# Layer 0's rows go back to their own order through a DRAM scratch and an accumulating indirect transfer

## The chip, the cores and the metric

The kernel runs on one core of a Trainium2 chip. The metric is the time of one execution on the device in microseconds (us), the median of several runs. Profiles come from one execution each.

## The reference

There are 128 graphs of 128 nodes with 64 features each, in float32, and two layers. `L0` and `L1` are the two networks below, and both layers use the same weighted adjacency:

```python
def L0(x, adj, W1, b1, W2, b2):
    mask = (adj > 0.0).astype(x.dtype)
    W1a, W1b = W1[:F], W1[F:]                    # F = 64, H = 192
    diff = x[:, :, None, :] - x[:, None, :, :]
    h = relu((x @ W1a)[:, :, None, :] + diff @ W1b + b1)
    hm = einsum('bjkh,bjk->bjh', h, mask)
    return hm @ W2 + mask.sum(-1)[..., None] * b2

def L1(feat, adj, W1, b1, W2, b2, W3, b3):
    agg = einsum('bmn,bnd->bmd', adj, feat)
    h = elu(agg @ W1 + b1)
    h = elu(h @ W2 + b2)
    return h @ W3 + b3

x = layernorm(x + L0(x, adj, ...))
x = layernorm(x + L1(x, adj, ...))
```

## The kernel before

**Tiling.** Two graphs make a pair, and there are 64 pairs (`NP`). Partitions are the 128 nodes, or 2 × 64 hidden channels of the two graphs. The adjacency has few entries in a row, so the kernel does not form all 128 × 128 differences. For each graph it ranks the nodes by the number of neighbours they have (`prepare`: `mk` is the mask, `pos` the rank of each node, `permb` the permutation matrix of it). It puts x into that sorted order with a matmul (`sort_x`) and also the mask (`sort_mask`). Then nine blocks of nodes (`BLOCKS`), each with a fixed number of neighbour slots, are worked off: in each unit ACT copies the node's own term `aj` into a PSUM bank `e` (L910), PE adds the neighbours' terms by 18 matmuls of one-hot matrices `oh` with `cp` (L920), and DVE sums absolute values over the slots into `sums` (L930). Four banks `e` are used in turn.

**The end of a pair** (`finish`). POOL forms `hm` from `sums` and a correction `corr` (L842). PE multiplies by W2 and adds the linear terms (L847, L851). ACT copies the result, in sorted order, to SBUF as `ys` (L855). PE brings the rows back to their own order by two float32 matmuls with the transposed permutation `permT` (L864). `permT` has been made in `sort_mask` by two matmuls of `permb` with an identity (L246, in the same PSUM bank as the sorted mask) and a copy on ACT (L661). Then `norm` adds x on DVE (`y`, L737), takes bn_stats (`st`, L742), makes the factors on POOL (`ve`, `rs`, `nb`, L749 to L753) and applies them on ACT to give `x1` (L771). Layer 1 follows: the product with the adjacency (L871), two hidden layers with elu on ACT and DVE (L791 to L797, L880, L886), the last matmul (L893), a second `norm` and the store of the output by SP (L897).

**What sets the order.** No engine's order is left to a scheduler at run time. All steps of all pairs are generators, and a small planner (`Flow`) calls them in the order of due times, which are written out by hand in a table `DUE`, in us of a plan with one round (one pair) per 11.1651 us. The entry of pair p is due at `ROUND * p` plus its number in the table. While the plan is under way, the step with the earliest due time is always issued next:

```python
            if self.under_way:
                t, th = min(ready, key=lambda r: self._rank(r[1]))
```

So the instructions of several pairs are interleaved in a fixed order on each engine. Waits are semaphores that the framework places where one engine uses what another has made.

Of the kernel before, what the change touches and what calls it, by code (L numbers as in the profile page):

```python
# [31 lines left out]
F32 = mybir.dt.float32  # L32
BF16 = mybir.dt.bfloat16
I32 = mybir.dt.int32
AF = mybir.ActivationFunctionType
OP = mybir.AluOpType
# [10 lines left out]
@with_exitstack  # L47
def gnn_kernel(ctx: ExitStack, tc: tile.TileContext, x, adj, w1, b1, w2, b2,
               v1, c1, v2, c2, v3, c3, out):
    nc = tc.nc  # L50
    B, N, F = x.shape
    H = w1.shape[1]
    O = w2.shape[1]
    H1 = v1.shape[1]
    P = 128
    HB = H // 3
    assert N == P and 2 * F == P and 2 * HB == P and H == 3 * HB and H1 == P and O == F and B % 4 == 0
    NP = B // 2

    LAY, E = [], 0  # L60
    for p0, p1, s in BLOCKS:
        n = s * (p1 - p0)
        assert 3 * n <= 512
        LAY.append((E, n, p0, p1, s))
        E += n
    NB = len(LAY)

    cpool = ctx.enter_context(tc.tile_pool(name="consts", bufs=1))
    ctx.enter_context(tc.manual_schedule())

    def const(shape, dt, name):
        return cpool.tile(shape, dt, name=name)


    degs = const([P, B], F32, "degs")

    with ExitStack() as fast:
        loads = fast.enter_context(tc.tile_pool(name="loads", bufs=8))
        prep = fast.enter_context(tc.tile_pool(name="prep", bufs=5))
        work = fast.enter_context(tc.tile_pool(name="work", bufs=5))  # L80
        ps_e = fast.enter_context(tc.tile_pool(name="ps_e", bufs=1, space=bass.MemoryType.PSUM))
        ps_m = fast.enter_context(tc.tile_pool(name="ps_m", bufs=1, space=bass.MemoryType.PSUM))
        K = sparse(tc, locals())
    with ExitStack() as slow:
        dense(tc, locals())
# [101 lines left out]
def sparse(tc, env):  # L187

    g = type("env", (), dict(env))
    nc, P, N, F, H, O, HB, H1, NP, E = (  # L190
        g.nc, g.P, g.N, g.F, g.H, g.O, g.HB, g.H1, g.NP, g.E)
    LAY, NB = g.LAY, g.NB
    loads, prep, work, ps_m = g.loads, g.prep, g.work, g.ps_m
# [3 lines left out]
    flow = Flow([ps_m.tile([P, 512], F32, name=f"m{i}") for i in range(4)])  # L197
    ADJ, XX, S = {}, {}, {}
# [3 lines left out]
    ROUND = 11.1651  # L202
    AHEAD = 4

    DUE = {
        "prepare": (-43.06, -42.93, -39.21, -39.08, -35.87),
        "sort_x": (-26.76, -10.46, -10.33, -3.14, -3.02, 2.5, 2.63, 2.76, 2.89),
        "sort_mask": (-26.12, -25.99, -25.86, -23.42, -23.29, -23.16, -13.67, -13.28, -13.03,
                      -12.77, -2.63, -2.25, -1.99, -1.73),
        "turn": (-36.9, -36.77),  # L210
        "project_c": (-32.15, -29.32, -29.2, -29.07, -28.94, -4.17, -4.04),
        "finish": (12.64, 19.44, 19.57, 21.62, 21.75, 21.88, 22.01, 28.04, 28.17, 29.2, 33.56,
                   33.69, 33.82, 34.71, 43.31, 43.44, 44.47, 44.6, 46.52, 46.65, 48.06, 48.19,
                   59.87),
        "unit": [(-1.48, 0.96, 1.09), (2.12, 2.25, 2.37), (3.02, 3.14, 3.27), (3.66, 3.79, 3.91),
# [1 line left out]
                 (7.25, 11.61, 11.74)],  # L217
    }

    def begin_thread(name, p, gen):  # L220
        flow.start(ROUND * p, DUE[name], gen)

    def event(*key):
        return EV.setdefault(key, [])

    def happened(ev, *key):
        event(*key)[:] = ev
# [5 lines left out]
    def act(n, pointers=0):  # L233
        return 0.07 + 0.09 * pointers + n / 1200

    def dve(n):
        return 0.08 + n / 960
# [12 lines left out]
    def flat(t):  # L250
        return t.rearrange("p s n -> p (s n)")
# [48 lines left out]
    rows = temp([P, NR], F32, "rows")  # L300
# [235 lines left out]
    def prepare(p):  # L536

        a = ADJ[p]
        d = S[p] = {}
        mk = d["mk"] = prep.tile([P, 2, N], BF16, name="mk")  # L540
        deg = g.degs[:, 2 * p:2 * p + 2]

        def count():
            for s in range(2):
                nc.vector.tensor_scalar(mk[:, s, :], a[:, s, :], 0.0, 0.0, op0=OP.is_gt,
                                        op1=OP.add, accum_out=deg[:, s:s + 1])
        ev, = yield ("DVE", 0.54, [event("load", p)], 0, count)
        degb = prep.tile([P, 2], BF16, name="degb")
        keyc = prep.tile([P, 2], F32, name="keyc")

        def keys():
            nc.gpsimd.tensor_copy(degb, deg)
            nc.gpsimd.tensor_sub(keyc, deg, jcol)
        ev, = yield ("POOL PORT", 0.32, [ev] + made("jcol"), 0, keys)

        def spread(key):
            for s in range(2):
                stationary(key[:, s * N:(s + 1) * N],
                           lambda h: degb[:, s:s + 1].to_broadcast([P, h.stop - h.start]),
                           identb, start=True, stop=True)  # L560
            stationary(key[:, 2 * N:3 * N], lambda h: small[:, h], iotb, start=True, stop=True)
        ev, key = yield ("PE:*", 0.17, [ev] + made("identb", "small", "iotb"), 1, spread)
        pos = prep.tile([P, 2], F32, name="pos")
        cmp = prep.tile([P, 2, N], BF16, name="cmp", bufs=3)

        def rank():
            for s in range(2):
                nc.vector.scalar_tensor_tensor(cmp[:, s, :], key[:, s * N:(s + 1) * N],
                                               keyc[:, s:s + 1], tie, op0=OP.subtract,
                                               op1=OP.is_gt, accum_out=pos[:, s:s + 1])  # L570
        ev, = yield ("DVE", 0.54, [ev] + made("tie"), 0, rank)
        permb = d["permb"] = prep.tile([P, 2, N], BF16, name="permb")

        def permute():
            nc.vector.tensor_tensor(permb, key[:, 2 * N:3 * N].rearrange("p (s n) -> p s n", s=1)
                                    .to_broadcast([P, 2, N]),
                                    pos.rearrange("p (s o) -> p s o", o=1).to_broadcast([P, 2, N]),
                                    op=OP.is_equal)
        ev, = yield ("DVE", 0.36, [ev], 0, permute)
        flow.give(key, ev)  # L580
        begin_thread("sort_x", p, sort_x(p, ev))
        begin_thread("sort_mask", p, sort_mask(p, ev))

    def sort_x(p, ev):

# [59 lines left out]
    def sort_mask(p, ev):  # L645

        d, a, permb = S[p], ADJ[p], S[p]["permb"]

        def sort(t):
            for s in range(2):  # L650
                stationary(t[:, s * N:(s + 1) * N], lambda h: d["mk"][:, s, h], permb[:, s, :],
                           start=True, stop=True)
            for s in range(2):
                stationary(t[:, (2 + s) * N:(3 + s) * N], lambda h: permb[:, s, h], identb,
                           start=True, stop=True)
        ev, t = yield ("PE:*", 0.22, [ev], 1, sort)
        mtp = d["mtp"] = prep.tile([P, 2, N], BF16, name="mtp", bufs=7)
        permT = d["permT"] = prep.tile([P, 2, N], F32, name="permT", bufs=7)
        evm, = yield ("ACT", act(2 * N), [ev], 0, lambda: nc.scalar.copy(flat(mtp), t[:, :2 * N]))
        happened(evm, "mtp", p)  # L660
        ev, = yield ("ACT", act(2 * N), [ev], 0, lambda: nc.scalar.copy(flat(permT), t[:, 2 * N:]))  # L661
        flow.give(t, ev)
        happened(ev, "permT", p)
        ev, vps = yield ("PE:*", 0.12, [evm] + made("prefix"), 1,
                         lambda vps: stationary(vps[:, :2 * N], lambda h: prefix[:, h], flat(mtp),
                                                start=True, stop=True))
        vp = prep.tile([P, 2, N], BF16, name="vp")
        ev, = yield ("ACT", act(2 * N), [ev], 0, lambda: nc.scalar.copy(flat(vp), vps[:, :2 * N]))  # L668
# [58 lines left out]
                     lambda: nc.gpsimd.tensor_sub(cp[:, 2], r1, cp[:, 1]))  # L727
        happened(ev, "cp", p)

    LATE = NP - 1  # L730

    def norm(p, yps, ev, name, rest, shift):


        y = work.tile([P, 2, O], F32, name="y", bufs=6)
        ev, = yield ("DVE", dve(2 * O), [ev], 0,
                     lambda: nc.vector.tensor_add(flat(y), yps[:, :2 * O], flat(rest)))  # L737
        flow.give(yps, ev)
        st = work.tile([P, 2, 3], F32, name="st", bufs=12)

        ev, = yield ("DVE", 0.2, [ev], 0,
# [93 lines left out]
    def finish(p):  # L835
# [19 lines left out]
        ev, = yield ("ACT", act(2 * O), [ev], 0, lambda: nc.scalar.copy(ys, yb[:, :2 * O]))  # L855
        flow.give(yb, ev)
        if p == NP - 1:
            due = DUE["finish"]
            flow.start(ROUND * p, [due[4]] * 4 + [due[8], due[12], due[12], due[14], due[15], due[15]],
                       overflow())  # L860

        def unsort(t):
            for s in range(2):
                nc.tensor.matmul(t[:, s * O:(s + 1) * O], d["permT"][:, s, :],  # L864
                                 ys[:, s * O:(s + 1) * O], start=True, stop=True)
        ev, t = yield ("PE", 0.4, [ev, event("permT", p)], 1, unsort)
        x1, ev = yield from norm(p, t, ev, "x1", xx, True)

        def aggregate(t):
# [309 lines left out]
```

## Time and profile before

| | |
|---|---|
| Median of three timed runs (lowest, highest) | 760.54 us (758.67, 761.2) |
| Span of the profiled execution, first to last instruction | 758.2 us |
| Granted TensorE clock, mean of the span | 0.988 |
| Busy share: PE, DVE, ACT, POOL | 97%, 95%, 93%, 57% |
| Matmuls L920 with the one-hot matrices | 393.3 us busy, 10368 of them |
| Matmuls L864 with `permT` | 256 passes, 275 ns median of one |
| Copies of `permT` (L661) on ACT | 64, 379 ns median of one |
| Sums `y` of layer 0 (L737) on DVE | 64, 276 ns median of one |
| First and last copy `ys` (L855) begin at | 47.5 us and 741.1 us |

The page gives the profiled execution by its span alone; the timed median is 2.3 us longer than that. Busy time counts an engine from the start of an instruction to its modelled end, and neighbouring instructions overlap by a few tens of ns in it. A line is that of kernel.py, where the instruction is recorded. In an answer by time, a row is start, duration, engine, line, operation, and in brackets the idle time ahead of it with the instruction that ended it.

### The profile page before, as it was taken

The page shows a single profiled execution, that of the slowest core. Times are in us where ns is not written, and L with a number is a line of the kernel's source. Part 1 is how long each engine was busy: PE and PEld are TensorE (multiplying, and loading weights), DVE is VectorE, ACT ScalarE, POOL GpSimd, SP SyncE. Part 2 cuts the span into 40 slices and gives each one's busy share as a digit, 9 for nine tenths or more (in the row PEclk, how much of TensorE's full clock was granted, in tenths as well). Part 3 has the DMA queues.
Part 4 walks back from the last instruction along what each step waited for, and adds up shares of the span by engine and source line. Part 5 has one row for each costly group of instructions (what it writes and reads, how often), then busy time and mean ns, then how long its engine had stood idle before and what let it go on. Part 6 is the DMA issues. An engine that isn't in the chain of part 4 may idle for free.

```text
span 758.2 us, 36118 instructions
## 1 busy us (share of the span) xinstructions
PE 736.3 (97%) x14788; PEld 672.4 (89%) x14789; DVE 722.5 (95%) x2381; ACT 705.7 (93%) x1986; POOL 432.4 (57%) x801
## 2 busy tenths in 40 slices
PE   7699999999999999999999999999999999999994
PEld 4588999999999999999999999999999999999993
DVE  7799999999999999999999999999999999999984
ACT  4499999999999999999999999999999999999984
POOL 5255566566556557556556656655655655655662
PEclk9799999999999999999999999999999999999998
DMA  4000011011011011011101101101101101100000
GB/s 121 15 3 3 17 31 31 17 31 32 16 31 32 20 27 31 20 27 31 28 20 31 31 17 32 31 16 31 31 20 28 31 21 27 31 21 16 10 13 19
DMA packets 54667, 19.72 MB, mean 26 GB/s; under 512 B 37600, under 2 KB 54496, under 8 KB 54496
## 3 DMA queue, kind: packets, MB, share of 16 engines
q1 hardware_dynamic: 53792, 17.05, 9.3%
q8 instruction: 118, 1.93, 1.1%
q14 instruction: 53, 0.43, 0.2%
q10 hardware_dynamic: 704, 0.30, 0.2%
HBM read 13.14 MB, written 4.19 MB: 23 GB/s over the span
## 4 chain that ended last, share of the span: by engine, by line
PE 95%; DVE 2%; ACT 1%; DMA 1%; issue 0%; POOL 0%; POOLq 0%; SPq 0%; DVEq 0%; ACTq 0%
PE e L920 46%; PE m L606 6%; PE m L708 5%; PE m L847 5%; PE m L886 4%; PE m L880 4%; PE m L893 4%; PE m L864 3%; PE m L246 3%; PE m L690 3%; PE m L592 2%; PE m L871 2%; PE m L851 1%; PE m L711 1%; PE m L248 1%; PE m L691 1%
## 5 line engine op out<-in xcount | busy, mean ns | idle before, releaser
L920 PE MATMUL e<-oh,cp 128*64 128x162 bf16 (+3 forms) x10368 | 393.3, 229 | 6.0 <-DVE oh L675 5.6
L920 PEld LDWEIGHTS <-cp 128*64 128x64 bf16 x10368 | 357.8, 110 | 18.3 <-issue 6.6
L930 DVE TENSOR_REDUCE sums<-e 128x54 f32<-128x486 f32 (+8 forms) x576 | 334.4, 608 | 10.2 <-PE e L920 4.6
L910 ACT COPY e<-aj 128x504 f32<-128x504 f32 (+6 forms) x576 | 293.6, 543 | 3.1 <-DVE sums L930 2.6
L749 POOL TENSOR_SCALAR ve<-st 128x2 f32<-128x2 f32 x126 | 24.1, 191 | 242.4 <-DVE st L742 237.0
L675 DVE TENSOR_TENSOR oh<-vp,slotc 128x308 bf16<-128x308 bf16 (+6 forms) x576 | 148.9, 315 | 4.8 <-ACT vp L668 1.3
L750 POOL TENSOR_TENSOR rs<-ve,mhalf 128x2 f32<-128x2 f32 x126 | 87.8, 697 | 10.5
L727 POOL TENSOR_TENSOR cp<-r,cp 128x512 bf16<-128x512 f32 x64 | 74.5, 1164 | 32.0 <-ACT cp L725 32.0
L642 POOL TENSOR_TENSOR corr<-ea,sa 128x384 f32<-128x384 f32 x64 | 64.3, 1005 | 16.5 <-DVE ea L635 11.5
L791 ACT ACTIVATE r<-m,cc 128x256 f32<-128x256 f32 x128 | 61.4, 480 | 5.2 <-PE m L880 3.2
L842 POOL TENSOR_TENSOR hm<-sums,corr 128x384 f32<-128x384 f32 x63 | 63.2, 1004 | 4.0 <-DVE sums L930 4.0
L620 POOL TENSOR_TENSOR sa<-aj,srow 128x384 f32<-128x384 f32 x64 | 64.3, 1005 | 1.0 <-ACT aj L613 1.0
L613 ACT ACTIVATE aj<-m,b1c 128x128 f32<-128x128 f32 x192 | 56.5, 366 | 8.2 <-PE m L606 1.2
L797 DVE SCALAR_TENSOR_TENSOR h<-m,cc,e 128x256 f32<-128x256 f32 x128 | 60.3, 471 | 2.0 <-ACT e L794 1.9
L794 ACT ACTIVATE e<-r 128x256 f32<-128x256 f32 x128 | 54.4, 426 | 2.1
L606 PE MATMUL m<-xsT,wad 128*128 128x128 f32 x384 | 53.7, 276 | 0.0
L847 PE MATMUL m<-w2d,hm 128*128 128x128 f32 x384 | 53.5, 276 | 0.0
L722 DVE TENSOR_TENSOR r<-m,cp 128x256 f32<-128x256 f32 x128 | 47.7, 414 | 1.6 <-ACT cp L718 1.6
L771 ACT ACTIVATE x<-y,nb,rs 128x64 f32<-128x64 f32 x126 | 49.0, 441 | 0.2 <-POOL nb L753 0.2
L718 ACT CAST cp<-m 128x256 bf16<-128x256 f32 x128 | 40.3, 366 | 8.8 <-PE m L711 8.8
L847 PEld LDWEIGHTS m<-w2d,hm 128*128 128x128 f32 x384 | 48.0, 192 | 0.3 <-POOL hm L842 0.3
L606 PEld LDWEIGHTS m<-xsT,wad 128*128 128x128 f32 x384 | 47.9, 192 | 0.4
(157 smaller groups left out, 1350.3 us busy)
## 6 DMA issues: line engine op xcount, KB each, us to landing
adj<-in_adj_dram SPq DMA_DIRECT2D x64, 128.0 KB, 2.9
xx<-in_x_dram SPq DMA_DIRECT2D x64, 64.0 KB, 2.6
out_dram<-o SPq DMA_DIRECT2D x64, 64.0 KB, 1.6
w1s<-in_L_gnn_W_dram ACTq DMA_DIRECT2D x2, 96.0 KB, 3.2
w2s<-in_L_gnn_W_dram ACTq DMA_DIRECT2D x2, 48.0 KB, 3.0
v2s<-in_L_gnn_W_dram SPq DMA_DIRECT2D x1, 64.0 KB, 2.2
v1d<-in_L_gnn_W_dram SPq DMA_DIRECT2D x2, 32.0 KB, 2.1
rows<-in_L_gnn_b_dram SPq DMA_DIRECT2D x1, 64.0 KB, 5.6
```

The lines of the kernel that those rows point to most:

```text
L606: nc.tensor.matmul(aps[:, c * N:(c + 1) * N], wad[:, c, :], xsT, start=True, stop=True)
L620: evs, = yield ("POOL PORT", 1.0, [have] + made("srow"), 0, lambda: nc.gpsimd.tensor_mul(sa, aj, srow))
L642: ev, = yield ("POOL PORT", 1.05, [ev, evs], 0, lambda: nc.gpsimd.tensor_sub(corr, ea, sa))
L675: lambda: nc.vector.tensor_tensor(oh[:, :, c].rearrange("p b (s w) -> p b s w", w=w), vp[:, :, p0:p1].rearrange("p b (o w) -> p b o w", o= ...
L727: lambda: nc.gpsimd.tensor_sub(cp[:, 2], r1, cp[:, 1]))
L750: nc.gpsimd.tensor_tensor(rs, ve, mhalf, op=OP.pow)
L791: lambda: nc.scalar.activation(r, z, AF.Relu, bias=c, scale=-1.0))
L842: lambda: (nc.vector if late else nc.gpsimd).tensor_sub(hm, d["sums"], d["corr"]))
L847: nc.tensor.matmul(yb[:, :2 * O], hm[:, c, :], flat(w2d[:, c]), start=(c == 0), stop=False)
L910: lambda: nc.scalar.copy(e.rearrange("p (c s w) -> p c s w", c=3, w=w), d["aj"][:, :, p0:p1].rearrange("p c (o w) -> p c o w", o=1) .to_br ...
L920: nc.tensor.matmul(e[s * HB:(s + 1) * HB, c * n:(c + 1) * n], cp[:, k, s, c * HB:(c + 1) * HB], oh[:, s, base:base + n], start=False, stop ...
L930: nc.vector.tensor_reduce(d["sums"][:, :, p0:p1], e.rearrange("p (c s w) -> p c w s", c=3, w=w), AX.X, OP.add, apply_absolute_value=True)
```

## The change

The rows of layer 0 of pairs 0 to 62 no longer pass through `permT`. SP writes `ys` to a scratch in DRAM, one tile for each of the two graphs. POOL then issues one indirect transfer for each graph, which fetches for node j the scratch row `pos[j]` and adds it to `xx[j]`, in SBUF, in the transfer itself. `norm` takes `xx` as its y and leaves its addition out. For these pairs `permT` is neither computed nor copied. A new step, `place`, turns the ranks into integers on POOL. The last pair (`LATE`) keeps the matmuls. The due times of `finish` change: the fetch is due at 22.3, bn_stats at 25.6 and the factors at 25.73, where the table had 21.62 (the matmuls), 21.75, 21.88 and 22.01; all later entries stay, so that x1 is due at 28.04 in both.

```diff
+        hbm = fast.enter_context(tc.tile_pool(name="hbm", bufs=4, space=bass.MemoryType.DRAM))
...
+        "place": (-34.9,),
-        "sort_mask": (-26.12, -25.99, -25.86, -23.42, ...
+        "sort_mask": (-26.12, -25.99, -23.42, ...
-        "finish": (12.64, 19.44, 19.57, 21.62, 21.75, 21.88, 22.01, 28.04, 28.17, 29.2, 33.56,
+        "finish": (12.64, 19.44, 19.57, 22.3, 25.6, 25.73, 28.04, 28.17, 29.2, 33.56,
...
+    DUE_LATE = {
+        "sort_mask": DUE["sort_mask"][:2] + (-25.86,) + DUE["sort_mask"][2:],
+        "finish": DUE["finish"][:3] + (21.62, 21.75, 21.88, 22.01) + DUE["finish"][6:],
+    }
+    LATE = NP - 1
...
+    def place(p, pos, ev):
+        at = S[p]["at"] = prep.tile([P, 2], I32, name="at", bufs=8)
+        ev, = yield ("POOL PORT", 0.15, [ev], 0, lambda: nc.gpsimd.tensor_copy(at, pos))
+        happened(ev, "at", p)
...
-            for s in range(2):
+            for s in range(2 if p >= LATE else 0):
                 stationary(t[:, (2 + s) * N:(3 + s) * N], lambda h: permb[:, s, h], identb,
...
-        ev, = yield ("ACT", act(2 * N), [ev], 0, lambda: nc.scalar.copy(flat(permT), t[:, 2 * N:]))
+        ev = evm
+        if p >= LATE:
+            permT = d["permT"] = prep.tile([P, 2, N], F32, name="permT", bufs=1)
+            ev, = yield ("ACT", act(2 * N), [ev], 0,
+                         lambda: nc.scalar.copy(flat(permT), t[:, 2 * N:]))
...
-        y = work.tile([P, 2, O], F32, name="y", bufs=6)
-        ev, = yield ("DVE", dve(2 * O), [ev], 0,
-                     lambda: nc.vector.tensor_add(flat(y), yps[:, :2 * O], flat(rest)))
-        flow.give(yps, ev)
+        if yps is None:
+            y = rest
+        else:
...
-        ev, t = yield ("PE", 0.4, [ev, event("permT", p)], 1, unsort)
+        if p < LATE:
+            rows = [g.hbm.tile([P, O], F32, name=f"rows{s}") for s in range(2)]
+            for s in range(2):
+                nc.sync.dma_start(rows[s], ys[:, s * O:(s + 1) * O])
+            def fetch_rows():
+                for s in range(2):
+                    nc.gpsimd.indirect_dma_start(
+                        xx[:, s, :], None, rows[s],
+                        bass.IndirectOffsetOnAxis(ap=d["at"][:, s:s + 1], axis=0), compute_op=OP.add)
+            ev, = yield ("POOL PORT", 1.6, [[ev[0] + 2.4], event("at", p)], 0, fetch_rows)
+            t, ev = None, [ev[0] + 2.4]
+        else:
+            ev, t = yield ("PE", 0.4, [ev, event("permT", p)], 1, unsort)
         x1, ev = yield from norm(p, t, ev, "x1", xx, True)
```

With these due times the order of POOL's instructions in a round becomes another. Pair numbers below are those of the pair whose result each instruction serves; q stands for whichever later pair is being prepared, and r for the older pair whose layer 1 ends:

```
before: hm(p)  degb keyc(q)  sa corr(q)  ve rs(r)  cp(q)  ve rs nb(p)
after:  hm(p)  degb keyc(q)  sa corr(q)  ve rs nb(p-1)  ve rs(r)  cp(q)  at(q)  fetch fetch(p)
```

In both kernels ACT applies x1(p-1) after two copies `e` of 504 and 462 elements and ahead of ys(p). On DVE, the bn_stats of layer 0 stand right behind `y` and ahead of an `h` (L797) in the kernel before, and behind `ea` (L635) in the changed one.

## The prediction

> **What bounds the kernel now.** I read the page's head first, then one steady stretch by engine, then the time order of two engines inside one round of that stretch.
>
> ```profile
> span 758.2 us, 36118 instructions
> ...
> PE 736.3 (97%) x14788; PEld 672.4 (89%) x14789; DVE 722.5 (95%) x2381; ACT 705.7 (93%) x1986; POOL 432.4 (57%) x801
> ```
>
> The window query (busy time by engine: PE, PEld, DVE, ACT, POOL, then the granted clock) gives for the middle of the run:
>
> ```profile
> 320.00:440.00 120.00, 120.00 (x2486) 110.79 (x2486) 117.95 (x387) 117.13 (x331) 71.53 (x128) 1.00 0.11 27
> ```
>
> TensorE has no gap at all. The chain that ended last is 95% PE, and the same PE pieces come back every 11.24 us (410.63, 421.87, 433.11 us), so a **round**, the work of one pair, costs 11.24 us of PE; DVE does 11.05, ACT 10.97, POOL 6.70 of work in it. On throughput PE is the bound and DVE is 0.2 behind. But every engine takes its instructions in a written order, so I look at that order too. POOL over one round (start, us, then operation, and in brackets the idle time before it):
>
> ```profile
> 409.62 1.01 POOL L842 TENSOR_TENSOR hm<-sums,corr 128x384 f32<-128x384 f32 x1
> 410.57 0.19 POOL L552 CAST degb<-degs 128x2 bf16<-128x2 f32 x1
> 410.71 0.20 POOL L553 TENSOR_TENSOR keyc<-degs,jcol 128x2 f32<-128x2 f32 x1
> 410.86 1.01 POOL L620 TENSOR_TENSOR sa<-aj,srow 128x384 f32<-128x384 f32 x1
> 411.95 1.01 POOL L642 TENSOR_TENSOR corr<-ea,sa 128x384 f32<-128x384 f32 x1
> 413.05 0.19 POOL L749 TENSOR_SCALAR ve<-st 128x2 f32<-128x2 f32 x1
> ...
> 414.41 1.16 POOL L727 TENSOR_TENSOR cp<-r,cp 128x512 bf16<-128x512 f32 x1 [0.39 <-ACT cp L725]
> 419.33 0.19 POOL L749 TENSOR_SCALAR ve<-st 128x2 f32<-128x2 f32 x1 [3.76 <-DVE st L742]
> 419.61 0.69 POOL L750 TENSOR_TENSOR rs<-ve,mhalf 128x2 f32<-128x2 f32 x1
> 420.40 0.50 POOL L753 TENSOR_SCALAR nb<-st,rs 128x1 f32<-128x1 f32 x2
> 420.86 1.01 POOL L842 TENSOR_TENSOR hm<-sums,corr 128x384 f32<-128x384 f32 x1
> ```
>
> To see: POOL's free time lies in one place, 3.76 us after cp, and layer 0's norm factors (ve, rs, nb at 419.33) come **before** the next pair's hm, keyc, sa and corr. And ACT between a pair's x1 and the next pair's ys:
>
> ```profile
> 411.58 0.78 ACT L771 ACTIVATE x<-y,nb,rs 128x64 f32<-128x64 f32 x2
> 412.25 1.06 ACT L910 COPY e<-aj 128x507 f32<-128x507 f32 x2
> ...
> 415.21 0.38 ACT L661 COPY permT<-m 128x256 f32<-128x256 f32 x1
> 415.47 0.50 ACT L695 COPY turned<-m 128x384 f32<-128x384 f32 x1
> ...
> 416.93 0.27 ACT L855 COPY ys<-m 128x128 f32<-128x128 f32 x1
> ```
>
> No bracket stands there: ACT is back to back for 5.62 us from the start of x1 to the end of ys (417.20).
>
> **What the skill says.** "DMA: Bandwidth & Descriptors", section "SWDGE vs HWDGE vs iDMA": an accumulating transfer can only be issued from GpSimd, which computes its descriptors in software. Its section "Latency and other measured facts" prices that at about 1 us to the first byte; no run here shows one yet. Its section "Two DMAs through the same engine are not ordered" says that a transfer that reads what another wrote has to wait for the other's completion semaphore, so POOL will sit on that wait. "TensorE: Matmul & The Clock Gate", section "Architectural detail: the array is 16× 32×32, not 1× 128×128", calls GpSimd a strict FIFO; the POOL rows above agree, since sa and hm never pass a waiting ve.
>
> **The change, part by part**, per round, for pairs 0 to 62.
>
> Removed from PE: the four L864 passes, 0.39 us in the chain of waits (417.52 to 417.91), and half of the eight L246 passes that turn mk and permb, 0.11. From ACT: permT, 0.26 from its start to the next. From DVE: y at L737, 0.28 (median 276 ns). That leaves PE 10.74, DVE 10.79, ACT 10.71.
>
> Added: on SP two row writes; the row `out_dram<-o SPq DMA_DIRECT2D x64, 64.0 KB, 1.6` is the nearest, 0.38 of queue time each. SP now uses 1.25 us in three issues, so it stays mostly empty; the output store and the loads queued behind the wait for ys are for four rounds ahead and keep several us (adj is issued at 410.64 and used at 421.09). POOL gets `at` (priced as degb, 0.19, hidden in the 3.76 us gap) and two indirect transfers, which wait for the writes.
>
> Moved, and this decides: in the changed kernel's POOL order each round reads cp, at, fetch, fetch, **hm, degb, keyc, sa, corr, then ve, rs, nb** of the pair just fetched, then the other norm's ve, rs. The bn_stats on DVE now stands behind ea. ACT keeps x1 at its old place, ahead of the next pair's ys. So a loop closes once per round: ys(p) → SP writes → POOL fetch(p) → hm to corr of the next pair → factors(p) → ACT x1(p) → ACT up to ys(p+1). Its length:
>
> - ACT, x1 to ys end, 5.62 − 0.26 (permT) = 5.36. PE's work in that stretch, from L871 to L851, is 3.58 without the removed transposes and ends no later.
> - ys to rows in DRAM: 1.6 by the out store, 0.05 for wake-up: 1.65. The second write, issued about 0.46 later, lands while the first fetch is being generated.
> - two fetches on POOL at 1.0 (the skill's price, taken because no row exists): 2.0. Bounds: 0.38 each (SP's issue of a plain transfer) to 2.0 each (twice the price).
> - hm to ve: 413.05 − 409.62 = 3.43.
> - ve to x1: ve to nb 1.07 (420.40 − 419.33), first nb to x1 0.30 (741.24 to 741.54 at the end of the run): 1.37.
>
> Sum 5.36 + 1.65 + 2.0 + 3.43 + 1.37 = **13.8 us** against 11.24. The fetched rows have 3.43 us to land and pass bn_stats (0.3) before ve; loads take 2.6 to 2.9, so this is just covered. If the accumulation takes 4 us, it adds 0.9. Below 11.2 us the loop would cost nothing, but 5.36 + 1.65 + 3.43 + 1.37 = 11.8 without any fetch at all, so the unknown cannot turn the sign by itself. The POOL waits also hold hm, keyc and cp back; hm is used by PE L847 five us after its present end, keyc by PE two us after, cp 3.6 us after, and all of these now move along with a longer round.
>
> The total: in the trace the first ys starts at 47.5 us and the last at 741.1, 63 intervals later, and 17.1 us follow. The early intervals, 10.2 to 10.7 us, become the loop's too, since its order is there from the first pair. The last five are 13 us shorter in sum than five rounds, as work of later pairs runs out; I keep 11 of that. 47.5 + 63 × 13.81 − 11 + 17.1 = 923.6 us of span. The page gives the profiled execution as its span of 758.2; the timed median is 2.3 above it (760.54), so **926**.
>
> **Rivals.**
> 1. The loop as above, 926. For it: the order is written out and engines do not reorder; each term but the fetch is measured.
> 2. A dearer loop: fetches at 2.0 us each, or TensorE's clock falling. The same TensorE page, section "Part 1: The HAM clock gate (the "warmup" mystery)", says an idle window of about 3.4 us halves it; PE will idle 13.8 − 10.7 = 3.1 us a round, in pieces. The head of the trace, where PE is not full, shows a mean clock of 0.87. At 15.8 us a round: 47.5 + 63 × 15.8 − 11 + 17.1 + 2.3 = 1051.
> 3. Faster: the round trip hides, POOL's gap of 3.76 us takes both fetches, and DVE becomes the bound at 10.79 plus its present 0.17 of gaps, about 10.9. 62 × 0.34 = 21 us saved: 739. It decides when write plus two fetches take less than 11.24 − 10.16 = 1.1 us (10.16 is the ACT and POOL part of the loop). The out store's 1.6 alone speaks against it.
> 4. No net change, 760: the loop comes out by chance at 11.2. It needs the ACT stretch to shrink by over half a us, which back-to-back work does not offer.
>
> **Chances.** Loop 0.80, dearer loop 0.16, faster 0.03, no change 0.01. A difference of 0.3% is about what a measurement of this kernel can tell. The range takes the fetch from about 0.5 us each (12.8: 862) to nearly 2.0 each: 860 to 1050.
>
> **What would show it.** Right: ys copies about 13.8 us apart; PE and DVE near 75 to 80% busy with their old durations; ACT waiting at x1 for POOL nb by 2 to 4 us per round; POOL waiting at the fetches for the rows' write; the chain of waits alternating between ACT and POOL with a DMA step of 1.6. Wrong: ys at 11 us or less, or DVE over 98%; a bn_stats that waits for the fetch long after corr has ended (then the landing is the term); POOL fetches far from 1 us.

## The result, and the profile after

| | before | after |
|---|---|---|
| Median of four timed runs (lowest, highest) | 759.65 us (758.67, 761.2) | 1162.7 us (1158.05, 1164.62) |
| Span of the profiled execution | 758.2 us | 1159.1 us |
| First and last copy `ys` begin at | 47.5, 741.1 us | 51.7, 1137.3 us |
| Mean round between these (63 of them) | 11.01 us | 17.23 us |

The changed kernel takes 1.53 times as long (95% interval 1.5264 to 1.5335). The forecast was 926 us, 860 to 1050: the sign was right, and the time lies far outside the range.

The head of the page of the changed kernel (busy time by engine, then the granted clock in 40 slices, in tenths):

```profile
span 1159.1 us, 35916 instructions
...
PE 856.8 (74%) x14300; PEld 744.7 (64%) x14301; DVE 723.5 (62%) x2318; ACT 692.1 (60%) x1923; POOL 647.7 (56%) x990
...
PEclk8889889888889889899889888888888898998895
```

No engine is over 75% busy, so none is full. PE issues 488 instructions fewer than before and is yet 120 us longer busy: its clock stands at 8 to 9 tenths over the whole span. The waits of the changed kernel, the longest totals (us in total, times, longest):

```profile
ACT x L794 <- POOL nb L776: 324.3, 62, 7.1
PEld m L907 <- ACT x L794: 235.5, 61, 4.9
PE m L907 <- ACT x L794: 225.6, 61, 4.7
POOL xx L896 <- DMA rows<-ys: 219.0, 45, 5.7
DVE st L765 <- DMA xx<-rows,at: 184.4, 58, 4.5
```

ACT's wait and PE's stand there about once per round. POOL's wait for the write of `ys` is named 45 times; in the other rounds the fetch also starts 2.2 us or more behind the issue of the write, but the profile names a PE instruction. Read as a ring they are the loop: ACT waits for POOL's `nb`, PE for ACT's x1, POOL for the write of `ys`. One round on POOL in the changed kernel (start, us, operation, idle time ahead of it):

```profile
505.89 0.18 POOL L600 CAST at<-pos 128x2 int32<-128x2 f32 x1
510.97 1.67 POOL L896 DMA_INDIRECT xx<-rows,at  x1 [4.90 <-DMA rows<-ys]
512.95 1.57 POOL L896 DMA_INDIRECT xx<-rows,at  x1 [0.30 <-PE m L648]
513.94 1.62 POOL L865 TENSOR_TENSOR hm<-sums,corr 128x384 f32<-128x384 f32 x1
...
516.85 0.99 POOL L661 TENSOR_TENSOR corr<-ea,sa 128x384 f32<-128x384 f32 x1
517.93 0.19 POOL L772 TENSOR_SCALAR ve<-st 128x2 f32<-128x2 f32 x1
518.21 0.72 POOL L773 TENSOR_TENSOR rs<-ve,mhalf 128x2 f32<-128x2 f32 x1
519.03 0.50 POOL L776 TENSOR_SCALAR nb<-st,rs 128x1 f32<-128x1 f32 x2
```

The place of `ve` is as forecast: behind hm, sa and corr, with no bracket, so it waits for nothing but its turn. Records of neighbouring POOL instructions overlap here (hm starts ahead of the end of the second fetch), so I count from start to start. The same round on ACT:

```profile
501.97 0.77 ACT L794 ACTIVATE x<-xx,nb,rs 128x64 f32<-128x64 f32 x2 [5.00 <-POOL nb L776]
...
506.07 0.37 ACT L677 CAST mtp<-m 128x256 bf16<-128x256 f32 x1 [0.87 <-PE m L257]
506.90 0.48 ACT L717 COPY turned<-m 128x384 f32<-128x384 f32 x1 [0.46 <-PE m L713]
507.61 0.88 ACT L632 ACTIVATE aj<-m,b1c 128x128 f32<-128x128 f32 x3 [0.22 <-PE m L625]
508.45 0.27 ACT L878 COPY ys<-m 128x128 f32<-128x128 f32 x1
...
519.33 0.77 ACT L794 ACTIVATE x<-xx,nb,rs 128x64 f32<-128x64 f32 x2 [5.03 <-POOL nb L776]
```

x1 to x1 is 17.36 us. Between x1 and ys there are now three short waits for PE, 1.55 us together, where the kernel before had none. PE in that stretch, below it the same 36 matmuls in the kernel before, then SP's issue of the writes (`x2` is the two of them) and the bn_stats on DVE:

```profile
502.46 0.76 PE L907 MATMUL m<-turned,x 128*64 128x128 f32 x4 [3.73 <-ACT x L794]
503.26 2.56 PE L956 MATMUL e<-oh,cp 128*64 128x169 bf16 x36
```
```profile
413.21 1.47 PE L920 MATMUL e<-oh,cp 128*64 128x169 bf16 x36
```
```profile
508.74 0.82 SPq L891 DMA_DIRECT2D rows<-ys  x2
```
```profile
516.46 0.30 DVE L765 BATCH_NORM_STATS2 st<-xx 128x6 f32<-128x128 f32 x1 [2.69 <-DMA xx<-rows,at]
```

PE is idle in one piece of 3.73 us ahead of the product that reads x1, and the 36 one-hot matmuls behind it take 2.56 us; the same 36 took 1.47 before. The granted clock says why. In the three stretches below (the piece, the time behind it, the rest of the round) it is the number behind the brackets of POOL: 1.00, 0.52, 1.00.

```profile
498.75:502.50 3.75, 0.04 (x1) 0.04 (x1) 3.37 (x9) 0.53 (x2) 3.25 (x7) 1.00 0.00 0
503.25:506.25 3.00, 2.98 (x42) 2.81 (x42) 1.01 (x2) 2.13 (x6) 1.29 (x2) 0.52 0.03 5
506.75:516.00 9.25, 8.85 (x177) 7.80 (x176) 5.75 (x21) 7.14 (x21) 4.72 (x6) 1.00 0.17 25
```

Read in steps of 0.25 us, the clock falls to 0.50 for spells of 3.41 us, in some rounds 6.83, around the end of this piece, and stands at 1.00 otherwise. The bn_stats waits for the landing of the fetch but is done by 516.76, 1.17 us ahead of `ve`: the landing is covered, as forecast.

The terms of the loop, forecast, measured in this round, and in the mean of 60 rounds (all but those at the start and the end):

| term | forecast | this round | mean of 60 | mean − forecast |
|---|---|---|---|---|
| ACT, start of x1 to end of ys | 5.36 | 508.72 − 501.97 = 6.75 | 6.65 | +1.29 |
| end of ys to first fetch | 1.65 | 510.97 − 508.72 = 2.25 | 2.53 | +0.88 |
| two fetches, then hm to ve | 2.0 + 3.43 | 517.93 − 510.97 = 6.96 | 6.97 | +1.54 |
| ve to x1 | 1.37 | 519.33 − 517.93 = 1.40 | 1.40 | +0.03 |
| sum | 13.81 | 17.36 | 17.55 | +3.74 |

The second row hides two kinds of rounds. In 48 of the 60 the fetch starts 2.2 us behind SP's issue of the write, in the other 12 between 2.7 and 4.4. In one of these, at 471.60 us, the writes themselves landed after 3.4 us (median of the two) in place of 1.5; why is open.

### The profile page after: what moved, and what is told of

The parts are those of the page before. It is cut to its first block, busy times and chain, and to the rows that moved or that the text cites. A ratio compares the mean times of both kernels' runs of the same rounds, so it can differ in the third digit from the quotient of the medians.

```text
span 1159.1 us, 35916 instructions
## 1 busy us (share of the span) xinstructions
PE 856.8 (74%) x14300; PEld 744.7 (64%) x14301; DVE 723.5 (62%) x2318; ACT 692.1 (60%) x1923; POOL 647.7 (56%) x990
## 4 chain that ended last, share of the span: by engine, by line
PE 56%; POOL 24%; DMA 6%; issue 5%; DVE 4%; ACT 4%; DVEq 0%; ACTq 0%; POOLq 0%; SPq 0%
PE e L956 24%; DMA xx<-rows,at 6%; POOL hm L865 5%; PE m L907 4%; PE m L625 4%; POOL xx L896 4%; POOL rs L773 4%; POOL corr L661 4%; PE m L730 4%; PE m L870 4%; POOL sa L639 3%; PE m L922 3%; PE m L916 3%; PE m L712 2%; PE m L929 2%
## 5 line engine op out<-in xcount | busy, mean ns | idle before, releaser
L956 PE MATMUL e<-oh,cp 128*64 128x162 bf16 (+3 forms) x10368 | 463.1, 251 | 2.8 <-ACT cp L747 0.7
L956 PEld LDWEIGHTS <-cp 128*64 128x64 bf16 x10368 | 421.1, 123 | 29.9 <-issue 16.0
L896 POOL DMA_INDIRECT xx<-rows,at x126 | 203.8, 1618 | 330.8 <-DMA rows<-ys 219.0
L794 ACT ACTIVATE x<-xx,nb,rs 128x64 f32<-128x64 f32 x126 | 48.6, 432 | 324.3 <-POOL nb L776 324.3
L907 PE MATMUL m<-turned,x 128*64 128x128 f32 x256 | 58.3, 378 | 225.6 <-ACT x L794 225.6
L907 PEld LDWEIGHTS m<-turned,x 128*64 128x64 f32 x256 | 29.8, 168 | 242.7 <-ACT x L794 235.5
L765 DVE BATCH_NORM_STATS2 st<-xx 128x6 f32<-128x128 f32 x63 | 18.7, 296 | 195.3 <-DMA xx<-rows,at 184.4
L749 POOL TENSOR_TENSOR cp<-r,cp 128x512 bf16<-128x512 f32 x64 | 73.9, 1155 | 109.2 <-ACT cp L747 102.3
L865 POOL TENSOR_TENSOR hm<-sums,corr 128x384 f32<-128x384 f32 x63 | 101.0, 1603 | 4.6 <-DVE sums L966 4.6
L639 POOL TENSOR_TENSOR sa<-aj,srow 128x384 f32<-128x384 f32 x64 | 100.4, 1568 | 2.4 <-ACT aj L632 2.4
L677 ACT CAST mtp<-m 128x256 bf16<-128x256 f32 x64 | 23.8, 372 | 53.9 <-PE m L257 53.9
```

Of the source, the lines that this page charges most:

```text
L639: evs, = yield ("POOL PORT", 1.0, [have] + made("srow"), 0, lambda: nc.gpsimd.tensor_mul(sa, aj, srow))
L865: lambda: (nc.vector if late else nc.gpsimd).tensor_sub(hm, d["sums"], d["corr"]))
L896: nc.gpsimd.indirect_dma_start(xx[:, s, :], None, rows[s], bass.IndirectOffsetOnAxis(ap=d["at"][:, s:s + 1], axis=0), compute_op=OP.add)
L907: nc.tensor.matmul(t[s * F:(s + 1) * F, :N], x1[:, s, :], d["turned"][:, s, :], start=True, stop=True)
L956: nc.tensor.matmul(e[s * HB:(s + 1) * HB, c * n:(c + 1) * n], cp[:, k, s, c * HB:(c + 1) * HB], oh[:, s, base:base + n], start=False, stop ...
```

## The experiments

Two questions: is it the **order** on POOL that closes the loop, or the latency of the transfers; and what **sizes** each term. A third set asks what the change could have brought.

### Is it the order?

**e1, no link from ys to the fetch.** Every fetch reads the rows of pair 0:

```diff
-                        xx[:, s, :], None, rows[s],
+                        xx[:, s, :], None, S[0]["rows"][s],
```

> Every pair's fetch reads the scratch rows of pair 0, so it does not wait for its own ys (the rows of later pairs are still written, and read by nobody; their layer-0 rows are therefore left out). All instructions, transfers and orders stay. Order theory (a loop ys - write - fetch - POOL's queue - x1 - next ys sets the round): the loop is cut between ys and fetch, the round falls from 17.2 us to that of the busiest engine, 10.8 to 11.4, and the run to 740-780 us. Rival, cost of the transfers themselves (descriptors on POOL, port or DMA contention): nothing changes in that, so the run stays above 1050 us.

Measured: 902.5 us in one run, a mean round of 13.14 us, granted clock 0.971. Neither range was met. Taking the link away gives 260 us back, but a loop stays, and POOL shows it:

```profile
504.08 1.16 POOL L749 TENSOR_TENSOR cp<-r,cp 128x512 bf16<-128x512 f32 x1 [1.54 <-ACT cp L747]
505.18 0.28 POOL L600 CAST at<-pos 128x2 int32<-128x2 f32 x1
505.63 1.67 POOL L899 DMA_INDIRECT xx<-first,at  x1 [0.17 <-issue]
...
514.18 0.50 POOL L776 TENSOR_SCALAR nb<-st,rs 128x1 f32<-128x1 f32 x2
...
517.30 1.16 POOL L749 TENSOR_TENSOR cp<-r,cp 128x512 bf16<-128x512 f32 x1 [1.56 <-ACT cp L747]
```

The fetch (of the tile now called `first`) no longer waits, but `cp` on POOL waits for a copy that ACT makes just behind x1, x1 waits for `nb`, and `nb` stands behind cp, at, both fetches and hm to corr. That is a second loop of 13.2 us that involves no ys at all. It lay in the shadow of the first, and its 1.55 us wait is there in the changed kernel too (its POOL cp waits 102.3 us in 62 times).

**e2, everything from bn_stats on one round later.** The due times change, the cyclic order on POOL hardly:

```diff
-        "finish": (12.64, 19.44, 19.57, 22.3, 25.6, 25.73, 28.04, ...
+        "finish": (12.64, 19.44, 19.57, 22.3) + tuple(
+            t + ROUND for t in (25.6, 25.73, 28.04, ...
```

> bn_stats, factors, x1 and all that follows are due one whole round (11.1651) later, so each serves the pair before; the cyclic order of instructions on every engine stays that of the changed kernel. Order theory: POOL's factors still stand behind this round's fetch and ahead of x1, which stands ahead of the next ys, so the loop closes as before through the queue although the data are a round old: 1120-1165 us. Rival, latency of the data (write, fetch, landing and statistics take longer than the round leaves between ys and x1): with 11 us more the wait is gone, below 820 us.

Measured: 1124.38 us in one run, round 16.64. A whole round more for the rows to come back buys 38 us. The fetch of p still stands ahead of the factors of an older pair, x1 of that pair ahead of the next ys, so the loop is closed by places in the queues, not by the time that the data need.

**e3, the factors ahead of the fetch in the round.** As e2, but bn_stats and factors at 33.2 and 33.3 in place of 25.6 + ROUND and 25.73 + ROUND.

> As the kernel with everything a round late, but bn_stats and the three factor steps of the pair before stand just ahead of the fetch on POOL instead of behind corr. Order theory: the loop now spans two rounds (about 18 us for two), and the next loop decides: PE's key matmuls L257 up to L874 and ys 4.3, write 2.25, two fetches 3.5, hm and the keys 1.4 = 11.5 us a round, 770-850 us. Rival, latency of the data: no different from the kernel with everything a round late.

Measured: 873.27 us in one run, round 12.67. Another place in the queue gives 289 us back with all transfers kept. It stays above the range that was expected, since now `degb` and `keyc` stand behind the fetches. The waits of e3, and its factors on POOL:

```profile
PE m L258 <- POOL degb L564: 88.6, 58, 2.6
```
```profile
515.93 0.19 POOL L773 TENSOR_SCALAR ve<-st 128x2 f32<-128x2 f32 x1 [1.68 <-DVE st L766]
```

PE needs the degrees to rank the next graphs, DVE compares what PE makes, the bn_stats stand behind that on DVE, and `ve`, which goes ahead of the next fetch, waits for them. Read from these waits, that is a third loop; e4 takes it away.

**e4, as e3, and degb and keyc ahead of the fetch.**

```diff
-        "prepare": (-43.06, -42.93, -39.21, ...
+        "prepare": (-45.3, -45.2, -39.21, ...
```

> As the kernel with the factors ahead of the fetch, and mk, degb and keyc are due 2.2 us earlier, so that POOL makes the keys ahead of the fetch too. Order theory: the loop that held the last one at 12.77 us a round (fetch, hm, keys on POOL; L258 on PE; cmp and, behind it in DVE's queue, bn_stats; then factors and fetch) is now spread over two rounds, as are all others that I can find (under 10 us a round); the bound is POOL's own work, 6.7 + 3.5 for the fetches + 0.3 for `at` and gaps between = 10.6 to 11.2 us, or DVE's 10.8: 735-780 us. Rival, the transfers slow the other engines or POOL itself beyond that (contention): 800 us or more.

Measured: 861.01 us (859.17 to 861.44), 1.1327 times before (1.1302 to 1.1351): in the rival's range, though the next lines speak against the rival's reason. The busy time between 200 and 600 us of e4 (PE, PEld, DVE, ACT, POOL, clock), and then one group on DVE as its page shows it (busy us, mean ns):

```profile
200.00:600.00 400.00, 371.01 (x7110) 322.85 (x7107) 392.12 (x1115) 340.11 (x953) 329.33 (x478) 0.99 0.18 34
```
```profile
L698 DVE TENSOR_TENSOR oh<-vp,slotc 128x308 bf16<-128x308 bf16 (+6 forms) x576 | 244.0, 485 | 0.5 <-PE e L957 0.5
```

PE's wait for `degb` is gone, and DVE is full, with the same 576 `oh` that took 315 ns each (148.9 us) before. They take 485 now, 95 us more of DVE. Where they lie says why. The kernel before on DVE, then DVE and POOL in e4:

```profile
416.80 1.91 DVE L675 TENSOR_TENSOR oh<-vp,slotc 128x338 bf16<-128x338 bf16 x7
```
```profile
502.18 2.71 DVE L698 TENSOR_TENSOR oh<-vp,slotc 128x338 bf16<-128x338 bf16 x7
```
```profile
502.04 0.71 POOL L774 TENSOR_TENSOR rs<-ve,mhalf 128x2 f32<-128x2 f32 x1
502.73 1.26 POOL L750 TENSOR_TENSOR cp<-r,cp 128x512 bf16<-128x512 f32 x1
```

The seven `oh` took 1.91 us before, when POOL stood in its gap; here they take 2.71, and rs and cp run beside them. The Trainium skill, "SBUF — State Buffer", section "Who interferes with whom", says that a VectorE operation with two inputs in SBUF contends with a GpSimd operation that reads SBUF. The traces agree and show a size. In e4 itself, 31 `oh` in groups with next to no POOL computation beside them take 0.26 us each from start to end of the group, and 473 in groups beside one for over 60% of their time take 0.44 (all widths of `oh` together). Beside POOL's indirect transfers alone they stay at 0.25 (407 of them in e11, below). So it is what POOL computes there that goes with the long `oh`, not the transfers. No run moved POOL's work alone, so that this is the whole cause of e4's length is argued.

### What sizes the terms?

**e5, PE kept warm.** Filler products into the bank of the product with x1, ahead of it, where PE idles in the changed kernel, for pairs 4 to 57:

```diff
+            for _ in range(14 if 4 <= p < NP - 6 else 0):
+                nc.tensor.matmul(t, identb, slotc[:, :512], start=True, stop=True)
```

> 14 extra bf16 matmuls of 512 columns into the bank of the aggregate, ahead of it, for pairs 4 to 57 (overwritten by it): some 3 us of work for PE where it waits 3.7 us for x1. Theory that the fall of PE's clock lengthens the stretch from x1 to ys (6.75 us against 5.36): the clock stays up, the stretch returns to about 5.4, the round to about 15.9, the run to 1075-1105 us. Rival, the stretch is long for another reason (the matmuls wait for ACT): 1150 us or more.

Measured: 1075.32 us in one run, mean round 15.87, clock 0.968 in the mean and 1.00 between 200 and 600 us. ACT in e5:

```profile
498.18 0.77 ACT L794 ACTIVATE x<-xx,nb,rs 128x64 f32<-128x64 f32 x2 [4.99 <-POOL nb L776]
...
503.07 0.27 ACT L878 COPY ys<-m 128x128 f32<-128x128 f32 x1
...
513.92 0.77 ACT L794 ACTIVATE x<-xx,nb,rs 128x64 f32<-128x64 f32 x2 [5.00 <-POOL nb L776]
```

x1 to the end of ys is 5.16 us (6.75 without the filler), x1 to x1 15.74, and nothing else in the loop moves: ACT's wait for `nb` is still 5.0. More work on an idle PE makes the kernel 87 us faster, so the clock is worth 1.4 us of the mean round and 1.6 between the two rounds shown. Rounds of one and the same kernel say the same: in e6, the next experiment, 21 rounds between 100 and 900 us have no spell of half clock in this stretch and take 5.16 to 5.17 us from x1 to the end of ys, and 26 have one whole spell of 3.41 us and take 6.14 to 6.76.

**e6, one fetch of the two** (`for s in range(1)`).

> The changed kernel with only one of the two indirect transfers of each pair; graph 1's layer-0 rows are left out of x1. The write of both stays. Theory that each fetch is a term of the loop by its time on POOL (1.97 from the first to the second): the round falls by 1.6 to 2.0 us, the run to 1035-1065 us. Rival, the fetches' time on POOL hides under the landing of the last one (DVE's bn_stats ends last): down by 0.5 us a round or less, 1125 us or more.

Measured: 1003.15 us in one run, mean round 14.78, clock 0.916. One fetch less is worth 2.45 us a round, more than the 1.6 to 2.0 that were expected. Over 60 rounds, first fetch to ve falls from 6.97 to 5.17 us, and x1 to the end of ys from 6.65 to 5.99, since fewer rounds see the slow clock. So the fetch itself answers for 1.80 of it, and the clock for 0.66.

**e7, the fetch without the addition** (`compute_op` left out).

> The changed kernel with the indirect transfers overwriting xx instead of adding to it: x is left out of layer 0's sum. Tells whether the accumulation is what makes the fetch dear. Loop theory: descriptors are made on POOL the same way; 1.6 us on POOL stay, and the landing is behind corr anyway: 1150-1165 us. Rival, the accumulation is the dear part (1.6 us on POOL and 3.4 to landing fall to 1.0 and 2.2): 1090 us or less.

Measured: 1104.16 us in one run, between the two. POOL in e7:

```profile
505.03 1.08 POOL L896 DMA_INDIRECT xx<-rows,at  x1 [5.64 <-DMA rows<-ys]
506.41 0.94 POOL L896 DMA_INDIRECT xx<-rows,at  x1 [0.30 <-issue]
507.38 1.02 POOL L865 TENSOR_TENSOR hm<-sums,corr 128x384 f32<-128x384 f32 x1
```

First fetch to hm is 2.35 us, where the adding one needs 2.97, and hm to corr 2.31 against 2.91; the record of one is 1.08 and 0.94 against 1.67 and 1.57. The DMA issues on the two pages, e7 first, show that landing is shorter as well (last number, us):

```profile
xx<-rows,at POOLq DMA_INDIRECT x126, 2.6
```
```profile
xx<-rows,at POOLq DMA_INDIRECT x126, 3.4
```

The mean round falls by 0.89 only (17.23 to 16.34). Over 60 rounds, first fetch to ve falls by 1.06 us (6.97 to 5.91), and x1 to the end of ys rises by 0.16 (6.65 to 6.81), with the clock at 0.851 in this run against 0.878. In the round shown ve also waits 0.21 us for the bn_stats, so with shorter fetches the landing begins to count:

```profile
510.89 0.19 POOL L772 TENSOR_SCALAR ve<-st 128x2 f32<-128x2 f32 x1 [0.21 <-DVE st L765]
```

**e13, a spare POOL product (128x384, reads what sa reads) between corr and ve, and e14, the same product behind nb.**

```diff
+            if shift:        # e13; in e14: if not shift:
+                nc.gpsimd.tensor_mul(spare, srow, srow)
```

> The changed kernel with one spare product of 128x384 (about 1.05 us) on POOL per pair between corr and layer 0's ve, which is inside the loop. Order theory: 1.05 us a round longer, and PE colder by a little: +60 to +110 us. Rival, POOL has 44% idle time and takes it up: less than +15 us.

> The same spare product behind layer 0's nb, ahead of layer 1's factors, where POOL waits 1.55 us for ACT's cp afterwards: outside the loop. Order theory: within 10 us of the changed kernel. Rival, POOL's work in sum counts, wherever it stands: as the kernel with the product inside the loop.

Measured: 1216.81 and 1159.84 us, one run each; +54 and −3 on the changed kernel, the first just below what was expected, the second within that kernel's own spread. In e13 it stands in the loop and costs its time every round: it takes 0.83 us, and the mean round grows by 0.88. In e14 it stands behind `nb`, and POOL's wait for ACT's copy shrinks for it, from 1.55 to 0.76:

```profile
502.51 0.83 POOL L774 TENSOR_TENSOR spare<-srow 128x384 f32<-128x384 f32 x1
...
505.17 1.16 POOL L750 TENSOR_TENSOR cp<-r,cp 128x512 bf16<-128x512 f32 x1 [0.76 <-ACT cp L748]
```

The same instruction on the same engine, 56% busy, is worth 57 us more in one place than in the other. That shows that the place between corr and ve lies in the loop, and the one behind nb does not.

### What could the change have brought?

**e10, only what the change removes**: no write, no fetch, no `at`; bn_stats and factors due as before.

> The removed work alone: permT, the unsorting matmuls and y are gone, as in the changed kernel, but no write, no `at`, no fetch; layer 0's result is left out of x1, and bn_stats and factors are at their due times of the kernel before. PE 10.74, DVE 10.79, ACT 10.71 us a round against 11.24: DVE sets 10.8 to 10.95, 735-742 us. Rival, the savings lie beside the path (PE's gaps are elsewhere): 755 us or more.

Measured: 731.75 us (731.61 to 731.9), 0.9632 times before (0.9615 to 0.9649), round in the middle 10.69 us. Layer 0's result is left out here. The removed work is thus worth 27.6 us, if the rows came back for nothing; the forecast's 10.74 for PE and 10.79 for DVE in a round were well sized. PE and DVE are then both full, in the window of e10:

```profile
200.00:600.00 400.00, 400.00 (x8370) 365.87 (x8368) 399.97 (x1311) 393.87 (x1125) 249.94 (x452) 1.00 0.11 28
```

**e11, all of the change, placed so that no loop closes**: the fetch at 21.2 + ROUND, bn_stats, factors, x1 and all later entries at their times of the kernel before + 2 ROUND (less for the last three pairs).

```diff
+        if name == "finish" and p < LATE:
+            back = NP - 1 - p
+            f, s = {1: (0.0, 5.0), 2: (0.5 * ROUND, ROUND), 3: (ROUND, 1.6 * ROUND)}.get(
+                back, (ROUND, 2 * ROUND))
+            due = due[:3] + (due[3] + f,) + tuple(t + s for t in due[4:])
```

> The change with three positions re-chosen, all results kept: the fetch of a pair one round later, right behind cp and `at`, so that POOL makes descriptors[...] while DVE compares oh; bn_stats, factors, x1 and all that follows two rounds later, at their places of the kernel before (the last three pairs less). Order theory with port contention as the second cost: every loop spans two or more rounds, oh is back near 315 ns, POOL's own work sets the round at about 11.0 us (fetches 3.5, at 0.3, the rest 6.7, gaps 0.4) or DVE's 10.8: 735-775 us. Rival, the fetches slow DVE's oh as well[...]: oh stays above 400 ns, 820 us or more.

Measured: 765.98 us (765.43 to 769.22), 1.0085 times before (1.0066 to 1.0104), round in the middle 11.11 us. With the same transfers, 397 of the 403 us are gone by due times alone. The same window of e11:

```profile
200.00:600.00 400.00, 398.14 (x8030) 363.01 (x8029) 393.82 (x1261) 385.46 (x1081) 364.30 (x541) 1.00 0.21 39
```

POOL has gone from 235.18 us before to 364.30, and PE and DVE are near full, at a longer round than in e10.

**e12, as e11, with a plain fetch into a tile of its own and the addition on POOL** (`tensor_add(y, yy, xx)`, 0.45 us).

> The same places, but the fetch copies into a tile of its own (0.95 to 1.1 us on POOL instead of 1.6) and POOL adds x afterwards (128x128, some 0.45 us), one round later, ahead of `at`. POOL's work per round falls by 1.1 - 0.45 = 0.6 us to about 10.4, so DVE (10.8) sets the round: 730-755 us, 5 to 20 below the version with the accumulating fetch. Rival, POOL is not the bound there and its reads of two more tiles cost DVE: equal or slower than that version.

Measured: 763.65 us (763.0 to 764.08), 1.0054 times before (1.0035 to 1.0074): 2 us below e11, not the 5 to 20 that were expected. Its mean round is 10.98 us against 11.01 before, which is 2 us in the run, while the first ys comes 3.8 us later and what follows the last ys takes 19.3 us in place of 17.1. So no version here that keeps the whole result beats the kernel before. Why the round is 11.1 in the middle of both and not e10's 10.69 is not settled: the nine `oh` of a round, at 341 ns in the mean in e11 and 323 in e12 against 315 before, explain 0.2 and 0.1 us of it.

## Why the prediction was right and wrong

**Right: the mechanism and the sign.** The loop ys → write → fetch → hm to corr → ve, rs, nb → x1 → ys is what the trace shows, with ACT waiting at x1 for `nb` and POOL at the fetch for the write. e2 shows that the order and not the latency closes it, e13 and e14 which of two places on POOL lies in it, e11 that it goes away with the order. The landing of the fetch, 3.42 us (512.95 to 516.37), was covered, as was said. The forecast that hm to ve and ve to x1 keep their length held within 0.03 us for the second; of the first only the sum with the fetches can be read.

**Wrong: the size, in three terms of the sum, all in the same direction.**

1. *Two fetches on POOL at 1.0.* If hm to ve kept its 3.43, they take 6.97 − 3.43 = 3.54, so 1.77 each. The price taken was a time to the first byte, used as the time that a fetch holds POOL; it is near e7's plain fetch (1.08 and 0.94), but the addition makes each 0.6 longer. The bounds held it, the point did not. 1.54 × 63 = 97 us.
2. *The ACT stretch kept at 5.36.* It was taken as ACT's own work, with PE at full clock. The clock's fall was put into a rival, because PE's idle time was thought to lie "in pieces". Nearly all of it lies in one piece, 3.73 of 4.13 us in the round shown: the product with x1 has one place in PE's written order, and PE waits there. The Trainium skill, "TensorE: Matmul & The Clock Gate", section "Part 1: The HAM clock gate (the "warmup" mystery)", puts the idle window that halves the clock at about 3.4 us. The traces agree on the halving, 1.00 to 0.50 for 3.41 or 6.83 us, but not on 3.4 us as the least idle piece: in e6 pieces of 2.4 to 2.5 us were followed by it in about half of the rounds, while in e7 six rounds with pieces of 3.08 to 3.56 had none of it between x1 and ys. At 1.45 us (e1) no spell came in 53 rounds. So the forecast's own idle time of 3.1 us a round could cost the clock, once it lay in one piece. e5 fills the piece and gets the clock and 5.16 us back. 1.29 × 63 = 81 us.
3. *The write priced by its landing, 1.6, and 0.05 for the wake-up.* The prediction counted this among the measured terms, but it was the landing of another transfer. That was well sized for the usual round (1.5 on the page), but POOL's fetch starts 2.2 us after SP's issue even then, and 2.7 to 4.4 after it in a fifth of the rounds. 0.88 × 63 = 55 us.

Together these are 233 us, against the 235.5 by which the span is longer than the forecast's 923.6. What is left nearly cancels: the first ys comes at 51.7 and not 47.5 (e10 has 51.1 without any transfer, so this comes from the new plan's start), the end takes 21.8 and not 17.1, and the first and last rounds are shorter than the steady ones by more than the 11 us that the forecast kept for the last.

**The range failed for its own reason.** It let one term be bad at a time: 2.0 for each fetch, *or* the clock. What came is the dearer loop, to which it gave a chance of 0.16, and with both at once. The two are not alternatives. A dearer fetch makes the round longer, and the longer round makes PE's idle piece longer (1.45 us in e1, 2.4 to 2.5 in most rounds of e6, 3.73 in the changed kernel), with which the clock between 200 and 600 us falls (1.00, 0.93, 0.89). The order isn't strict: e7, with pieces mostly of 3.1, has 0.85. The upper end should have added 2.0 for the fetches, the cold PE and the slower hand-over: 13.81 + 2.0 + 1.4 + 0.6 = 17.8 us a round, which by the forecast's formula is about 1178 us.

**The faster rival** was rightly kept small. It named a round trip of at most 1.1 us as the point from which it decides; the hand-over and the fetches alone are 5.8 in the round shown.

## What to carry to other kernels

When a step that waits moves onto an in-order engine, write that engine's new cyclic order down and follow the ring: who waits for the instruction behind the waiting one, and where does that engine's queue come back to the start. Its length is then a sum of all terms, and its terms are linked: slack that a loop made on TensorE gathered at one wait here, and cost the clock as well. And behind one loop lay others (rounds of 17.2, 13.1 and 12.7 us in the changed kernel, e1 and e3). Before giving such a change up, try its due times: the same transfers cost 403 us in one order and 7 in another, but even a free round trip could bring only the 27.6 us that the removed work was worth.

## What the runs showed of the hardware that was not expected

- An accumulating indirect transfer (128 rows of 256 bytes) holds POOL for about 0.6 us longer than a plain one: 1.97 us from the first to the second in the changed kernel and e11, 1.38 and 1.39 in e7 and e12. It also lands later behind the same order (3.4 against 2.6 us, the changed kernel and e7), though hardly in the order of e11 and e12 (3.2 against 3.1).
- PE's granted clock falls from 1.00 to 0.50 for spells of 3.41 us, or 6.83, around idle pieces of PE of 2.4 to 2.5 us (e6), in about half of the rounds there; pieces of 1.45 us (e1) brought none. Filling the piece with products nobody reads brings 1.00 in e5.
- `oh` on DVE (two bf16 inputs in SBUF) takes 0.44 us beside POOL's computations and 0.26 without them (e4), and 0.25 beside POOL's indirect transfers (e11).
- After SP's issue of a 32 KB write, a waiting POOL instruction starts at 2.2 us in 48 of 60 rounds, 0.7 later than the landing that the page gives.
